# Decay attention in a sixteen-layer hybrid network: the norm and routing steps in other slots

## The chip, the cores and the metric

The program runs on one core of one Trainium2 chip. The metric is the device time of one execution in microseconds (us). Times come as a median over runs, and one execution was recorded by the hardware profiler. The engines are TensorE (PE, with its weight loads listed as PEld), VectorE (DVE), ScalarE (ACT), GpSimd (POOL) and SyncE (SP), which issues most of the transfers. Each engine takes its instructions in program order and waits on semaphores for the others.

## The reference, cut to what matters

The network has sixteen layers. Each one adds `f(layernorm(x))` to `x`, where `x` holds 4096 tokens of 128 channels. The change concerns the decay attention (layer 1, part b) and, inside its loop, the first half of the mixture of experts (MoE) that follows it.

```python
# decay attention: 16 heads of 8 channels, groups of T = 256 tokens
q = (x @ Wq.T + bq).reshape(B, T, H, hd)          # k and v likewise
scores = jnp.einsum('bqhd,bkhd->bhqk', q, k) * scale
decay = jnp.exp(-alpha * jnp.abs(idx[:, None] - idx[None, :]) * DT)
attn = jax.nn.softmax(scores * decay, axis=-1)
out = jnp.einsum('bhqk,bkhd->bqhd', attn, v).reshape(B, T, D)
return out @ Wo.T + bo
...
# the MoE that follows: the best 2 of 8 experts for each token
logits = jnp.einsum('nc,ec->ne', xt, gate_w)
top_vals, top_idx = jax.lax.top_k(logits, TOP_K)
top_w = jax.nn.softmax(top_vals, axis=-1)
```

## The kernel before, in words

`x` lies in SBUF with channels on partitions and is worked on in 8 chunks (`NCH`) of 512 tokens; a chunk holds two groups of 256 tokens. `decay` (L2952) prepares data and a list of steps, and hands them to `small_stage` (L2797), which writes the order of every engine by hand: it counts slots, and what it records in a slot goes into the engines' queues in just that order. Nothing is reordered later.

**One item per slot.** A chunk has 8 items, two groups times four blocks of 128 queries by 128 keys, so item n of chunk c is slot n = 8c to 8c+7. In slot n the loop records, in this order:

1. `score(n)`: four matmuls on PE into four PSUM banks, then `evict` (L2970). For an even slot VectorE multiplies the four banks by the decay table (`pt<-ps,dec`) and the exponential over the whole tile is left for the next slot. For an odd slot ScalarE takes the exponential straight from the four banks (`pt<-ps`). The odd slots take queries and keys that GpSimd has scaled before (`qx`, `kx`).
2. The exponential left from slot n-1 (`pt<-pt`, on ScalarE, so always in an odd slot).
3. The steps that have become due in this slot (`later`, L2816). Where several are due, the leading steps described below come first, then `join`, `turn` and `out`.
4. `weigh_by_head(n-3)`: 32 small matmuls with the values. After each second item the result is copied out as `raw`, by ScalarE or VectorE in turn, always in an even slot. It is transposed and divided (`turn`, `rd` and `o`) one slot later. The two halves are brought together (`join`, `ot`) and, for the second group, multiplied by Wo and added to x by VectorE (`out`, L2905) in slot 8c+13.
5. The steps of chunks to come: `project` (q and k) at 8c-6, `values` at 8c-5, `queries` at 8c-4 and 8c (`qz`), `keys_by_edge` (`kx`) at 8c-3, `queries_by_edge` (`qx`) at 8c-2 and 8c+2, `guard` (two reductions, `peaks`) at 8c+1, and three steps of the norm of x (`norm_x_step`, L1811): a centring matmul with a copy on ScalarE and a square on GpSimd; a mean matmul with a logarithm and an exponential on ScalarE (`nrs`); the scaling on VectorE (`ha<-ha,nrs`). Chunks 0 to 4 were normed by the stage before, so here only chunks 5 to 7 have these three.

PE takes its banks from a ring of six ("s") for everything but the weighing, so that a matmul waits until the bank used six allocations earlier has been read.

**The leading steps.** The stage after the attention is the MoE, so `out(c)` also makes due the eleven steps of `Sending.steps` (L3639) for its chunk, one per slot in the kernel before: three of the norm (centre with copy and square on ScalarE; `nrs` on ScalarE; `ha` on VectorE), `compare` (L3660, a matmul for the logits, then VectorE), `choose` (L3679, thirteen small VectorE instructions), `place` (L3707, small matmuls and five VectorE instructions), `turn` (L3730, four transposes and two copies on ScalarE into `out`), and four `scatter` steps (L3739) of two indirect DMAs each, recorded on GpSimd (L3743). With the last chunk's steps the loop runs on after the last item, up to slot 80. Then `table` is made and the stage of the experts begins; its first `x<-rows` transfer on SP's queue reads what the scatters wrote.

PE's order is therefore fixed in each slot: a matmul that waits for VectorE or ScalarE also holds everything recorded behind it.

Of the kernel before, what the change touches and what calls it, by code (L numbers as in the profile page):

```python
# [21 lines left out]
NCH = NT // CH  # L22
# [1627 lines left out]
class Fast(Net):  # L1650
# [1143 lines left out]
            w["bv"].rearrange("p (h d) -> p h d", h=16)[:, None].broadcast_to([P, 4, 16, 8]), ALU.add,  # L2794
        )

    def small_stage(self, w, units, steps, tiles, evict, finish=None, group=1):  # L2797

# [7 lines left out]
        with ExitStack() as st:  # L2808
            p = self.stage(st, "sm", 1)
# [1 line left out]
            pts, po, ots, os, rests, due = {}, {}, {}, {}, {}, {}  # L2811
            lead = self.lead(p, "s", spread=True)
            first = min(at for at, _ in steps) - 3 * group
            steps = [(first + i * group, lambda c, i=i: self.norm_x_step(p, c, i, "s")) for i in range(3)] + list(steps)

            def later(n, i, f, c):  # L2816


                for _ in range(i):
                    n += 1 if group == 1 or n % group < group - 2 else group - n % group  # L2820
                due.setdefault(n, []).append((order.index(f) if f in order else 0, f, c))
# [13 lines left out]
            def weigh(n, slot):  # L2835
                c, b, it, jt, kind = items[n]
                vz = tiles(c, b, it, jt)[2]
                if n % len(units) == 0:
                    po[0] = self.bank("o")
                pt = pts.pop(n)  # L2840
                first, last = n % len(units) == 0, n % len(units) == len(units) - 1
                for u in range(4):
                    for r in range(4):
                        cc = slice(32 * r, 32 * r + 32)
                        nc.tensor.matmul(
                            po[0][cc, it * P : it * P + P], vz[:, u, cc], pt[:, r, u], start=first and u == 0,
                            stop=last and u == 3, skip_group_check=True,
                        )
                if last:
                    if b == 0:  # L2850
                        ots[c] = p.tile([P, CH], F32, tag="ot", name="ot", bufs=2)
                    finish(c, b, ots[c][:, b * T : b * T + T], po[0])
                    if b == 1:
                        later(slot, 1, out, (slot, c))
# [38 lines left out]
            def join(args):  # L2893
                slot, n = args
                c, b, *_ = items[n]
                if b == 0:
                    ots[c] = p.tile([P, CH], F32, tag="ot", name="ot", bufs=2)
                pt = self.bank("s")
                for it in range(2):
                    self.tr(pt[:, it * P : it * P + P], os.pop((c, b, it)))  # L2900
                self.act(ots[c][:, b * T : b * T + T], pt[:, :T], AF.Copy)
                if b == 1:
                    later(slot, 3, out, (slot, c))

            def out(args):  # L2905
                slot, c = args
                pz = self.bank("s")
                self.mm(pz, w["Wo"], ots.pop(c))
                x = self.x[:, self.chunk(c)]
                if "bo" in w:  # L2910
                    self.stt(x, pz, w["bo"], x, ALU.add, ALU.add)
                else:
                    self.tt(x, x, pz, ALU.add)
                for i, f in enumerate(lead):
                    later(slot, (2 if finish else 4) + i, f, c)

            order = [None, join, turn, out]
            with self.share(s=6, o=2), self.tc.manual_schedule():
                self.logs()
                n = first  # L2920
                while n < len(items) + 3 * group or due:
# [13 lines left out]
                    for at, f in steps:  # L2935
                        c, u = divmod(n - at, many)
# [15 lines left out]
    def decay(self, w):  # L2952


        h0 = self.ha
        nc = self.nc
        with ExitStack() as st:
            p1 = self.stage(st, "d1", 1)
            p2 = self.stage(st, "d2", 2)
            na = p1.tile([P, 1], F32, tag="na", name="na")  # L2960
            self.ts(na, w["alpha"], -1.0, ALU.mult)
            dec = p1.tile([P, P], F32, tag="dec", name="dec")
            self.act(dec, w["lag"][:, :P], AF.Exp, scale=na)
            edge = p1.tile([P, T], F32, tag="edge", name="edge")
            self.act(edge, w["edge"], AF.Exp, scale=na)
            bad = p1.tile([P, 1], F32, tag="bad", name="bad")
            self.ts(bad, w["alpha"], 0.0, ALU.is_lt, 1e30, ALU.mult)
            vzs = self.with_ones(p1, 2)

            def evict(kind, pt, ps):  # L2970
                if kind:
                    for r in range(4):
                        self.act(pt[:, r].rearrange("p h t -> p (h t)"), ps[r], AF.Exp, scale=8.0**-0.5)
                    return
                for r in range(4):
                    self.tt(pt[:, r], ps[r].rearrange("p (h t) -> p h t", h=4), dec[:, None, :].broadcast_to([P, 4, P]), ALU.mult)
                flat = pt.rearrange("p r h t -> p (r h t)")
                return lambda: self.act(flat, flat, AF.Exp, scale=8.0**-0.5)

            qs, ks, kxs, qzs, qxs = {}, {}, {}, {}, {}  # L2980

            def project(c):
                for n, held in (("q", qs), ("k", ks)):
                    pq = self.bank("s")
                    self.mm(pq, w["W" + n], h0[:, self.chunk(c)])
                    held[c] = p2.tile([P, CH], F32, tag=n, name=n)
                    self.act(held[c], pq, AF.Identity, bias=w["b" + n])

            def values(c):
                self.values_by_head(w, vzs[c % 2], self.chunk(c))  # L2990

            def queries(c, b):
                qzs[c, b] = self.masked_copy(p1, qs[c], b)

            def keys_by_edge(c):
                kxs[c] = p2.tile([P, CH], F32, tag="kx", name="kx")
                self.gt(self.bt(kxs[c]), self.bt(ks[c]), self.twice(edge), ALU.mult)

            def queries_by_edge(c, b):
                qxs[c, b] = p1.tile([P, 4, T], F32, tag="qx", name="qx", bufs=3)  # L3000
                self.gt(qxs[c, b], qzs[c, b], edge[:, None, :].broadcast_to([P, 4, T]), ALU.mult)

            def guard(c):
                self.guard(DECAY, c, qs[c], ks[c])
                if c == 0:
                    at = DECAY * 2 * PEAKS
                    self.tt(self.peaks[:, at : at + 1], self.peaks[:, at : at + 1], bad, ALU.add)

            def tiles(c, b, it, jt):
                kk, qq = (ks, qzs) if it == jt else (kxs, qxs)  # L3010
                j = b * T + jt * P
                return kk[c][:, j : j + P], qq[c, b][:, :, it * P : it * P + P], vzs[c % 2][:, 2 * b + jt]

            steps = [
                (1, guard), (-6, project), (-5, values), (-4, lambda c: queries(c, 0)), (-3, keys_by_edge),
                (-2, lambda c: queries_by_edge(c, 0)), (0, lambda c: queries(c, 1)), (2, lambda c: queries_by_edge(c, 1)),
            ]
            units = [(0, 0, 0), (0, 1, 1), (1, 1, 0), (1, 0, 1)]
            self.small_stage(w, units, steps, tiles, evict)

    def guard(self, stage, c, q, k):
        self.peak(stage, 0, c, q)
# [823 lines left out]
```

## Time and profile before

| | |
|---|---|
| median of 3 runs | 4256.13 us (4253.08 to 4257.88) |
| profiled execution | 4251.58 us, of it span 4249.8 us |
| decay attention with its leading steps | about 2200 to 2514 us of the span |
| `peaks<-q` of chunks 2 to 7 (slot 8c+1) starts at | 2265.45, 2299.67, 2337.21, 2374.87, 2412.54, 2446.74 us |
| one `qx` on GpSimd | 2.37 us |
| one `rows<-out,idx` issue on GpSimd | 0.97 to 1.05 us, 1.27 from start to start |

The distance between two `peaks<-q` is the time of one chunk in the steady part of the loop: 34.22 us, 37.54, 37.66, 37.67 and 34.20. The three longer ones hold the norm of chunks 5, 6 and 7. In a timeline each line gives the start, the length, the engine, the line of the kernel and operation, and in brackets the idle time of that engine just before with what ended it; lines of one kind are merged, so the idle time inside a merged line is not shown, and its length shows it instead.

### The profile page before, as it was taken

To read this page: it belongs to the slowest core of one execution; us is meant where nothing else is said; L and a number is where in the kernel's file an instruction comes from. 1 tells how busy PE (TensorE), PEld (TensorE's weight loads), DVE (VectorE), ACT (ScalarE), POOL (GpSimd) and SP (SyncE) were. 2 spreads that over 40 slices of the span, in tenths; PEclk is the share of its full clock that TensorE was granted. 3 is DMA by queue.
4 is the path that set the end of the run, shared out by engine and by line. 5 is a ranking of instruction groups with operands and counts; after the bars stand their busy time and mean duration, and the time that the engine had idled before them with its cause. 6 is when DMAs were issued, how large, how long until landed. Compare 5 with 4: busy or idle time off the path is not lost. (4 is left out here: it accounts for less than half of the span.)

```text
span 4249.8 us, 73853 instructions
## 1 busy us (share of the span) xinstructions
PE 3860.8 (91%) x28998; PEld 2207.7 (52%) x28998; DVE 2557.6 (60%) x4503; ACT 2327.2 (55%) x4741; POOL 1852.0 (44%) x1632
## 2 busy tenths in 40 slices
PE   7999999998899999995989979888999999899878
PEld 3555466464465456553965459643444344455333
DVE  4775577364477477555336643565788687486474
ACT  6665466554766456553447634444555455774432
POOL 4664365232565166316433334454555455311251
PEclk9999999988999999997999979999999999999989
DMA  1800000000000000002930049100000000000000
GB/s 61 343 1 1 11 1 1 20 1 1 20 1 1 1 4 2 1 1 83 330 125 12 17 137 316 61 19 16 1 1 1 3 1 1 16 2 18 6 0 21
DMA packets 78404, 176.43 MB, mean 42 GB/s; under 512 B 12606, under 2 KB 39108, under 8 KB 77920
## 3 DMA queue, kind: packets, MB, share of 16 engines
q1 hardware_dynamic: 65568, 148.40, 10.1%
q0 software_dynamic: 9120, 18.51, 1.2%
q8 instruction: 231, 3.78, 0.4%
q10 hardware_dynamic: 3360, 4.72, 0.3%
q14 instruction: 125, 1.02, 0.1%
HBM read 118.28 MB, written 54.20 MB: 41 GB/s over the span
## 5 line engine op out<-in xcount | busy, mean ns | idle before, releaser
L528 ACT ACTIVATE pt<-ps 128x512 f32<-128x512 f32 x640 | 340.0, 600 | 327.7 <-PE ps L504 326.4
L504 PE MATMUL ps<-hb,w 128*128 128x512 f32 (+1 forms) x960 | 458.7, 611 | 6.9 <-issue 3.3
L504 PE MATMUL ps<-w,hb 128*128 128x512 f32 (+2 forms) x896 | 403.4, 571 | 27.9 <-DVE t L531 20.9
L534 POOL TENSOR_TENSOR t<-t,t 128x512 f32<-128x512 f32 x256 | 319.3, 1268 | 160.8 <-DVE t L531 101.2
L531 DVE TENSOR_TENSOR t<-ps,tab 128x512 f32<-128x512 f32 x512 | 317.5, 681 | 83.8 <-ACT sq L528 80.3
L534 POOL TENSOR_TENSOR t<-t,ss 128x1024 f32<-128x1024 f32 x128 | 243.5, 1903 | 218.9 <-ACT ss L528 217.6
L504 PEld LDWEIGHTS ps<-hb,w 128*128 128x128 f32 (+1 forms) x960 | 178.0, 190 | 263.7 <-issue 224.3
L528 ACT ACTIVATE qkt<-ps 128x512 f32<-128x512 f32 x256 | 140.5, 595 | 309.0 <-PE ps L508 308.4
L531 DVE TENSOR_TENSOR u<-u,ps 128x384 f32<-128x384 f32 (+1 forms) x206 | 121.8, 595 | 287.9 <-PE ps L508 182.9
L531 DVE TENSOR_TENSOR ot<-ps,rd 128x512 f32<-128x512 f32 (+2 forms) x224 | 143.2, 639 | 232.0 <-ACT rd L528 232.0
L534 POOL TENSOR_TENSOR nsq<-ha 128x512 f32<-128x512 f32 x112 | 122.9, 1097 | 320.4 <-ACT ha L528 308.6
L504 PEld LDWEIGHTS ps<-w,hb 128*128 128x128 f32 x896 | 155.5, 192 | 185.4 <-issue 113.6
L534 POOL TENSOR_TENSOR both<-pt 128x1024 f32<-128x1024 f32 x64 | 151.2, 2362 | 200.0 <-DVE pt L531 164.3
L504 PE MATMUL ps<-nsq,ct 128*128 128x512 f32 x368 | 201.0, 629 | 36.0 <-POOL nsq L534 32.1
L504 PE MATMUL ps<-ot,w 128*128 128x512 f32 x448 | 213.6, 611 | 16.8 <-DVE ot L531 9.0
L504 PE MATMUL ps<-xt,w 128*128 128x128 f32 x1704 | 221.0, 280 | 1.5 <-ACT xt L528 1.5
L2199 POOL DMA_INDIRECT back<-y,x x142 | 138.9, 978 | 184.2 <-ACT y L528 90.4
L504 PE MATMUL ps<-u,w 128*128 128x512 f32 (+1 forms) x448 | 215.4, 605 | 3.4 <-POOL u L534 3.4
L528 ACT ACTIVATE u<-ps,w 128x512 f32<-128x512 f32 x160 | 107.8, 685 | 183.8 <-PE ps L504 181.3
L504 PEld LDWEIGHTS ps<-xt,w 128*128 128x128 f32 x1704 | 204.8, 194 | 2.9 <-ACT xt L528 2.9
L528 ACT ACTIVATE nrs<-ps,ct 128x512 f32<-128x512 f32 x208 | 139.8, 683 | 101.8 <-PE ps L504 95.9
L3743 POOL DMA_INDIRECT rows<-out,idx x128 | 125.8, 982 | 155.1 <-ACT out L528 105.7
(362 smaller groups left out, 8937.9 us busy)
## 6 DMA issues: line engine op xcount, KB each, us to landing
w<-in_moe_x SPq DMA_DIRECT2D x142, 533.0 KB
rows<-t SPq DMA_DIRECT2D x64, 520.0 KB
x<-rows SPq DMA_DIRECT2D x142, 65.0 KB
w<-in_local_f SPq DMA_DIRECT2D x8, 659.5 KB
y<-back ACTq DMA_DIRECT2D x16, 256.0 KB
y<-back SPq DMA_DIRECT2D x16, 256.0 KB
w<-in_local_f SPq DMA_DIRECT2D x4, 658.5 KB
back<-y,x POOLq DMA_INDIRECT x142
```

Source lines behind the costliest of these rows:

```text
L504: self.nc.tensor.matmul(out, lhsT, rhs, start=start, stop=stop)
L528: self.nc.scalar.activation(out, in_, func, **kw)
L531: self.nc.vector.tensor_tensor(out, a, b, op)
L534: self.nc.gpsimd.tensor_tensor(out, a, b, op)
L2199: nc.gpsimd.indirect_dma_start(views[i], bass.IndirectOffsetOnAxis(ap=x[:, C : C + 1].bitcast(I32), axis=0), y, None, bounds_check=2 * NT ...
L3743: nc.gpsimd.indirect_dma_start(views[(c * 2 + k) * 4 + t], bass.IndirectOffsetOnAxis(ap=idx[:, k, t : t + 1], axis=0), out[:, k, t], None,)
```

## The change

`small_stage` takes two further arguments. `norm_at` names the slots of the three norm steps (before: three consecutive slots ending with the one before the earliest step, 8c-9, 8c-8, 8c-7; now 8c-10, 8c-8, 8c-7). `lead_at` names the distance of each of the eleven leading steps from the slot in which the chunk's last item is weighed, 8c+10 (before: 4 to 14, one slot after the other). It holds for chunks 0 to 6; the last chunk keeps the old distances. Only `decay` hands them over. In slots: norm of the MoE 8c+14, 16, 17 (before 14, 15, 16), `compare` 19 (17), `choose` 21 (18), `place` 23 (19), `turn` 24 (20), scatters 25 to 28 (21 to 24). No instruction is added or taken away.

```diff
-    def small_stage(self, w, units, steps, tiles, evict, finish=None, group=1):
+    def small_stage(self, w, units, steps, tiles, evict, finish=None, group=1, norm_at=None, lead_at=None):
...
             first = min(at for at, _ in steps) - 3 * group
-            steps = [(first + i * group, lambda c, i=i: self.norm_x_step(p, c, i, "s")) for i in range(3)] + list(steps)
+            norm_at = norm_at or [first + i * group for i in range(3)]
+            first = min(norm_at)
+            steps = [(norm_at[i], lambda c, i=i: self.norm_x_step(p, c, i, "s")) for i in range(3)] + list(steps)
...
                 for i, f in enumerate(lead):
-                    later(slot, (2 if finish else 4) + i, f, c)
+                    later(slot, lead_at[i] if lead_at and c < NCH - 1 else (2 if finish else 4) + i, f, c)
...
-            self.small_stage(w, units, steps, tiles, evict)
+            self.small_stage(
+                w, units, steps, tiles, evict, norm_at=(-10, -8, -7), lead_at=(4, 6, 7, 9, 11, 13, 14, 15, 16, 17, 18),
+            )
```

## The prediction

> **What bounds the kernel now.** The page first, for the engines over the whole span; then busy time by stretches of 34 us, about one chunk; then PE's timeline of the loop, and VectorE's and GpSimd's beside it where PE stands still.
>
> ```profile
> PE 3860.8 (91%) x28998; PEld 2207.7 (52%) x28998; DVE 2557.6 (60%) x4503; ACT 2327.2 (55%) x4741; POOL 1852.0 (44%) x1632
> ...
> 2302.00:2336.00 34.00, 31.08 (x370) 17.36 (x373) 21.23 (x52) 23.86 (x38) 15.31 (x12) 0.95 0.05 17
> ```
>
> PE leads everywhere: 31.08 of 34 us here, VectorE 21.23, ScalarE 23.86. But "busy" includes matmuls held up between their parts, so I price each slot's work from starts in undisturbed slots: score 1.07 us, weighing 1.01, turning `raw` 0.53, join 0.37, Wo 0.96, the two norm matmuls 1.05 and 0.96, logits 0.9, place 0.35, the MoE's turn 0.5, projection 1.92, values 1.07. Eight scores, eight weighings, four turns, two joins and one of each other make 27.3 us per chunk, against 34.2 from `peaks<-q` to `peaks<-q`. Seven us are lost, and they sit in few places. With s for slot modulo 8, this is s = 2 and 3 of chunk 3, PE's timeline:
>
> ```profile
> 2301.72 2.78 PE L504 MATMUL ps<-qx,kx 32*128 32x512 f32 x8
> 2304.89 0.19 PE L504 MATMUL ps<-both,before 128*128 128x32 bf16 x1 [0.40 <-DVE both L538]
> 2304.93 0.32 PE L504 MATMUL ps<-both,ones 128*128 128x24 bf16 x7
> 2306.96 0.91 PE L508 MATMUL ps<-ct,raw 128*128 128x128 f32 x4 [1.71 <-ACT pt L528]
> 2307.80 1.94 PE L2866 MATMUL ps<-pt,vo 128*32 128x128 f32 x32
> 2309.66 1.58 PE L504 MATMUL ps<-w,ha 128*128 128x128 f32 x8
> 2311.17 1.14 PE L504 MATMUL ps<-qz,k 32*128 32x512 f32 x8
> ```
>
> From 2301.72 to 2311.17 are 9.45 us for 4.03 us of work (1.07+0.35+0.53+1.01+1.07). VectorE and GpSimd at that time:
>
> ```profile
> 2296.55 1.92 DVE L531 TENSOR_TENSOR ahead<-lg 128x256 f32<-128x256 f32 x1
> ...
> 2300.85 2.47 DVE L531 TENSOR_TENSOR pt<-ps,dec 128x512 f32<-128x512 f32 x4
> 2303.24 0.41 DVE L3683 TENSOR_REDUCE rank<-ahead 128x32 f32<-128x256 f32 x1
> ...
> 2306.13 0.69 DVE L639 COPY raw<-ps 128x512 f32<-128x512 f32 x1
> ...
> 2295.82 2.37 POOL L534 TENSOR_TENSOR qx<-qz,edge 128x1024 f32<-128x1024 f32 x1 [2.71 <-ACT pt L528]
> ```
>
> `compare` (s=1) makes the even slot's eviction late, so the odd slot's fourth bank comes free late; then `choose` (2303.24 to 2306.13, 2.9 us) stands before the copy of `raw`, and PE waits for that copy. The bracket names ScalarE's `pt`, but the copy ends just before. Afterwards PE is slow for some 4 us (weighing 1.94 for 1.08). The loss is 5.4 us.
>
> Two smaller losses stand where a chunk is normed, three times:
>
> ```profile
> 2329.49 1.12 PE L504 MATMUL ps<-nsq,ct 128*128 128x512 f32 x2 [0.82 <-POOL nsq L534]
> ...
> 2337.43 1.96 PE L504 MATMUL ps<-ha,w 128*128 128x512 f32 x4 [0.98 <-DVE ha L531]
> ```
>
> [...] `ahead` takes 1.92 us under `qx` and 0.42 otherwise, ending 0.28 us after it. [...] about 2.1 us idle, then 4 us slow. [...]
>
> **The change, part by part.** No instruction changes; the order of all engines but SP does.
>
> *Removed (A).* `choose` leaves the even slots, and `compare` leaves s=1, where it met `qx`. Five times 9.38 to 9.45 us for 4.03 are 5 x 5.4 = 27.0. A sixth (2446.88 to 2456.85, 9.97 us, own work 2.96 as it has no values) gives 7.0. Together 34.0.
>
> *Removed (B).* The norm's centring goes two slots ahead of its mean, and `compare` no longer stands before its scaling: 3 x 0.82 and 0.98+1.10+1.11 = 5.6.
>
> *Removed (C).* s=0 is so short (2.45 us) that the next score waits for a bank: 4.39 us for 3.53 at 2293.33, three times, 2.4. In the new order s=0 also has the turn and the mean, 3.9 us. Removed in all: 42.0.
>
> *Added (a): ScalarE in s=0 and 1.* s=0 now holds the MoE's `out` (0.97 from start to start), `nrs` (0.74+0.54), `ot` 0.3, `raw` 0.5, `qz` 0.8. With t0 the start of s=0's score, ScalarE is still at s=7's exponentials until t0+2.15, so `raw` ends at t0+5.25, and turning it, at t0+4.98 on PE, waits 0.47; s=1's evictions start at t0+6.0 and the next score's fourth bank costs 0.2. With the chunk's own `nrs` (1.3 more) the evictions start at about t0+7.3, after which the bank costs 0.9. Two chunks at 0.7 and three at 0.9: 4.1.
>
> *Added (b): `choose` in s=5* stands before `turn`'s and `out`'s VectorE work. It starts after s=4's eviction and `qz`, 4.15 us after s=4's score begins (1.15 until the banks are full, 2.4, 0.6). Its 2.9, then `rd`, `o` (0.5) and the addition to x (0.75) end at 8.3. s=6's score begins at 6.7 (2.45 and 0.7 bank wait for s=4, 3.54 for s=5), so the centring matmul could go at 7.77 and waits some 0.65. Behind it on PE stand the weighing and all of s=7. And `qx` (due in s=6) starts as soon as that `qz` is done, where before it was queued behind scatters: it holds `choose`'s `tensor_tensor`s until 2.37+0.28 us later, 1.5 us on top. In the three chunks with a norm (slots 29, 37, 45) GpSimd's `nsq` is queued ahead of `qx` and waits for s=6, so there is no meeting; slot 61 has no `qx` any more. So 4 x 0.65 and 2 x 2.2 = 7.0. After 2.2 us idle PE may be slow: nothing to 1.4 each (0.9 on the weighing, 0.5 on the values, above); I take 0.7, as the gap is one and not two: 1.4.
>
> *Added (c).* `compare` now meets the last pair (slot 59), which has no projection to cover it; a bank wait of 0.6 stays.
>
> *Added (d): the tail.* After the last item chunk 7's chain sets the end:
>
> ```profile
> 2483.91 0.97 POOL L3743 DMA_INDIRECT rows<-out,idx  x1 [14.29 <-ACT out L528]
> ...
> 2493.29 0.63 ACT L528 ACTIVATE nrs<-nrs 128x512 f32<-128x512 f32 x1
> ...
> 2502.81 0.96 POOL L3743 DMA_INDIRECT rows<-out,idx  x1 [9.03 <-ACT out L528]
> ...
> 2514.30 0.35 SPq L2165 DMA_DIRECT2D x<-rows  x1
> ```
>
> Chunk 6's scatters started at 2483.91 and were over before chunk 7's at 2502.81; the first `x<-rows` waits for the last. Now chunk 6's `turn` is in slot 72, behind chunk 7's `nrs` (over at 2493.9). `compare` in slot 67 also costs some 1.2 us ahead of `rd`. So GpSimd starts at about 2496.1 and has 16 issues at 1.27, to 2516.4, instead of 2512.7: 3.7 us, which nothing covers, because SP's loads for the experts are in line behind that `x<-rows`. `choose` and `place` of chunk 6 fit into the tail's idle VectorE (3.1 us before the addition, 6.8 before `ha`).
>
> The extra first slot (-10) is empty for chunk 0, normed earlier: nothing.
>
> Sum: 42.0 - (4.1+7.0+1.4+0.6+3.7 = 16.8) = 25 us less. Against the profiled execution 4251.6 - 25 = 4226.6; the median of the runs stands 4.5 above it, so 4231.
>
> **Rivals.**
> 1. *The delay moves from s=3 to s=6.* `choose` is held by `qx` in all six chunks and PE goes slow each time: 6 x (2.2+1.4) = 21.6 in place of 8.4, gain 12, 4244. For it: `qx` now follows `qz` at once. Against: `nsq` ahead of it in three chunks.
> 2. *(a) and (b) are hidden by slack I don't see*: only (c), (d) and the 0.65s stay, 42.0-0.6-3.7-2.6 = 35, 4221. For it: ScalarE has 10 us free per chunk.
> 3. *Slower.* If GpSimd comes late to `kx`, `kx` (1.27) and `qx` hold `choose` one after the other: 0.65+1.27+2.37+0.28 = 4.6 us idle before the centring, then twice the slow stretch's 1.4: 7.4 per chunk, 44.4 in all. With (a), (c), (d), 8.4, that is 10.8 more than removed: 4267. It decides from 5.6 us per chunk on (33.6/6). Against: `kx` needs k, done two slots earlier, and the scatters end before.
>
> **How the numbers follow.** The forecast has 0.65 (about 4222 to 4241), rival 2 0.12, rival 1 0.14, rival 3 0.09. A measurement of this kernel can tell about 0.2%, 8.5 us. Rival 1 lies half within that bound: faster 0.65+0.12+0.06 = 0.83, same 0.08, slower 0.09. The range goes down to 4215, past rival 2, as (a) and (b) could vanish whole, and up to 4247, rival 1 with half a us more in each of six chunks; what is left out is rival 3 and the edges. The forecast's own range is 4222 to 4241.
>
> **What would show it.** `peaks<-q` distances of about 31 to 32 us in all steady chunks; at s=3 a score of 1.14 us and no wait for `raw`; on PE a wait for `x` ahead of the centring matmul, longer where `choose` lies under `qx`; the first `x<-rows` 16 scatters after chunk 7's `nrs`. Wrong if s=6 loses over 5 us per chunk, or if ScalarE's `pt` starts more than 3 us after s=1's score.

## The result, and the profile after

| | before | after |
|---|---|---|
| median | 4256.45 us (4 runs, 4253.08 to 4257.88) | 4230.2 us (4 runs, 4228.95 to 4232.05) |
| profiled execution | 4251.58 us | 4230.16 us |
| first score of the attention to the score of slot 63 | 263.4 us | 232.1 us |
| slot 63's score to the first `x<-rows` | 46.9 us | 48.3 us |
| sum of the eight slots s = 3 | 64.0 us | 33.7 us |
| sum of the eight slots s = 6 | 24.0 us | 33.3 us |

The ratio is 0.994, with a 95% interval of 0.9928 to 0.9952: 26 us less. A "slot" is measured from the start of PE's score to the start of the next one. By the trace the stage became 29.9 us shorter, but the profiled executions differ by only 21.4: the after execution reached the first score 8.3 us later, through stages in which nothing had changed. In a second pair of profiles it reached it 1.5 us earlier, so this is scatter between executions. The profiled "before" lay 4.9 us under the median of its runs. The stage is therefore compared from its own first score throughout.

The engines' busy times of the page, and a window of 32 us that is about one chunk (span, then busy us and instruction counts of PE, PEld, DVE, ACT and POOL, then clock, DMA share and GB/s):

```profile
PE 3853.1 (91%) x28998; PEld 2201.8 (52%) x28998; DVE 2557.5 (60%) x4503; ACT 2326.0 (55%) x4741; POOL 1854.5 (44%) x1632
...
2337.00:2369.00 32.00, 31.30 (x384) 16.91 (x383) 25.21 (x61) 25.22 (x40) 15.10 (x12) 1.00 0.06 19
```

Instruction counts and the engines' shares of the span are those of before. The change hardly shows here: over the whole span PE's "busy" falls by 7.7 us, because it was 13.5 us higher ahead of the stage. From the first score to the first `x<-rows` it falls from 263.8 to 244.9 us; matmuls that were stretched by a wait, or ran slowly after one, had counted as busy (of the 4.21 us from 2306.96 to 2311.17 in the profile before, 4.21 are busy, at a mean clock of 0.59). The change shows in the timeline of the slot that had taken 9.45 us, s = 3 of chunk 3, PE:

```profile
2306.10 1.14 PE L504 MATMUL ps<-qx,kx 32*128 32x512 f32 x8
2307.17 1.06 PE L504 MATMUL ps<-w,ha 128*128 128x8 f32 x8
2308.08 0.63 PE L508 MATMUL ps<-ct,raw 128*128 128x128 f32 x4
2308.65 1.08 PE L2868 MATMUL ps<-pt,vo 128*32 128x128 f32 x32
2309.66 1.16 PE L504 MATMUL ps<-w,ha 128*128 128x128 f32 x8
2310.74 1.14 PE L504 MATMUL ps<-qz,k 32*128 32x512 f32 x8
```

No bracket is left: each matmul follows the one before it. The score takes 1.14 us where it took 2.78, there is no wait for `raw`, and the weighing is at 1.08 instead of 1.94. The slot is 4.64 us for 4.64 us of work. All five such slots read 4.65.

What was paid for it stands in s = 6, here chunk 2, PE, then VectorE and GpSimd:

```profile
2286.52 1.14 PE L504 MATMUL ps<-qz,k 32*128 32x512 f32 x8
2289.70 1.13 PE L504 MATMUL ps<-x,ct 128*128 128x512 f32 x2 [2.03 <-DVE x L543]
2290.75 1.08 PE L2868 MATMUL ps<-pt,vo 128*32 128x128 f32 x32
...
2284.97 1.70 DVE L531 TENSOR_TENSOR rank<-rank,won 128x32 f32<-128x32 f32 x1
...
2288.90 0.74 DVE L543 SCALAR_TENSOR_TENSOR x<-ps,w,x 128x512 f32<-128x512 f32 x1
...
2284.25 2.37 POOL L534 TENSOR_TENSOR qx<-qz,edge 128x1024 f32<-128x1024 f32 x1 [6.84 <-DVE qz L538]
```

`rank<-rank,won` is 128 x 32 elements and takes 0.19 us elsewhere. Here it takes 1.70: it started while `qx` ran and ended just after it (2286.67 against 2286.62). Everything behind it is 1.5 us late, so x too, and PE waits for x. Slot 54 is as long (5.24 us, as here); in the three chunks with a norm it is about 0.5 us, and in slot 62 next to nothing.

### The profile page after: what moved, and what is told of

It is laid out like the page before. It is cut to its first block, busy times and chain, and to the rows that moved or that the text cites. A ratio compares the mean times of both kernels' runs of the same rounds, so it can differ in the third digit from the quotient of the medians.

```text
span 4228.4 us, 73859 instructions
## 1 busy us (share of the span) xinstructions
PE 3853.1 (91%) x28998; PEld 2201.8 (52%) x28998; DVE 2557.5 (60%) x4503; ACT 2326.0 (55%) x4741; POOL 1854.5 (44%) x1632
## 5 line engine op out<-in xcount | busy, mean ns | idle before, releaser
L504 PE MATMUL ps<-nsq,ct 128*128 128x512 f32 x368 | 203.1, 635 | 31.7 <-POOL nsq L534 27.3
L504 PE MATMUL ps<-ha,w 128*128 128x512 f32 x320 | 178.5, 680 | 11.7 <-ACT f L528 10.2
```

The costliest lines, as they stand in the source:

```text
L504: self.nc.tensor.matmul(out, lhsT, rhs, start=start, stop=stop)
```

## The experiments

The first four ran on a chip on which the kernel before took 4280.8 us (median of 37 runs); for the others it took 4253.4 and 4254.7. All edits are against the kernel after; "before again" is the kernel before with four more lines that do nothing. `lead_at` holds the distances from slot 8c+10, so its fifth entry, 11, is the choice in slot 8c+21 (s = 5). "Loop" is first score to slot 63's score, "end" is from there to the first `x<-rows`.

| kernel | loop, us | end, us | median, us | ratio to before (95%) |
|---|---|---|---|---|
| norm half alone | 272.5 | 45.0 | 4275.54 | 0.9989 (0.9981 to 0.9998) |
| routing half alone | 262.3 | 55.7 | 4275.34 | 0.999 (0.9981 to 0.9999) |
| choice in s4 | 246.8 | 54.7 | 4260.84 | 0.9953 (0.9939 to 0.9967) |
| choice in s6 | 270.0 | 58.5 | 4288.73 | 1.0021 (1.0013 to 1.0028) |
| before again | 264.3 | 44.1 | 4253.91 | 1.0 (0.9992 to 1.0009) |
| after again | 231.7 | 48.3 | 4223.84 | 0.9933 (0.9916 to 0.995) |
| choice in s7, placing in s1, turn in s2, tail | 239.7 | 45.5 | 4231.14 | 0.9948 (0.9931 to 0.9965) |
| chunk 6 on old distances ("tail") | 231.8 | 45.3 | 4220.59 | 0.9924 (0.9906 to 0.9943) |
| norm half alone, again | 262.9 | 47.6 | 4255.94 | 1.0002 (0.9995 to 1.0008) |
| routing half alone, again | 237.1 | 48.7 | 4230.96 | 0.9945 (0.9927 to 0.9963) |
| tail, turn in s2 | 231.1 | 44.3 | 4221.11 | 0.9924 (0.9908 to 0.9941) |
| tail, choice in s4 | 228.7 | 47.9 | 4221.11 | 0.992 (0.9903 to 0.9937) |

### The halves on the first chip

```diff
 norm half alone
-                w, units, steps, tiles, evict, norm_at=(-10, -8, -7), lead_at=(4, 6, 7, 9, 11, 13, 14, 15, 16, 17, 18),
+                w, units, steps, tiles, evict, norm_at=(-10, -8, -7),
 routing half alone
+                w, units, steps, tiles, evict, lead_at=(4, 6, 7, 9, 11, 13, 14, 15, 16, 17, 18),
```

> Only the chunk's own norm steps stand in the new slots (8c-10, 8c-8, 8c-7); the eleven leading steps stay one per slot as before. Theory (the gain comes from VectorE's choose and compare leaving the places ahead of work that PE waits for): only the three waits of 0.82 us for nsq go, 2 to 4 us less than before, and the slots 8c+3 stay at about 9.4 us. Rival (the norm steps carry the gain): 10 us or more less than before.

> Only the leading steps stand in the new slots; the chunk's own norm stays at 8c-9, 8c-8, 8c-7. Theory: almost all of the gain, but qx is now queued on GpSimd ahead of nsq in the three chunks with a norm, so that it holds choose there too: slots 30, 38 and 46 (the own norm's centring is not in them any more) show a wait for x of about 2 us in place of 0.5, 4.5 us more than the whole change, some 22 us less than before. Rival (nsq's place in GpSimd's queue has nothing to do with it; the hold is something else): those slots wait 0.5 us as in the whole change, and the time is that of the whole change within 2 us.

The norm's half gained 5 us, with an interval from 1 to 8. The routing's half gained 5 us as well, far too little. Its trace has idle time of PE that the profiles of before and after do not have. PE in the end part of the routing half, while GpSimd issues its scatters:

```profile
2490.59 2.80 PE L2868 MATMUL ps<-pt,vo 128*32 128x128 f32 x49
2494.36 0.44 PE L2868 MATMUL ps<-pt,vo 128*32 128x128 f32 x5 [0.97 <-issue]
2495.79 0.43 PE L2868 MATMUL ps<-pt,vo 128*32 128x128 f32 x4 [1.00 <-issue]
2497.21 1.10 PE L2868 MATMUL ps<-pt,vo 128*32 128x128 f32 x4 [0.99 <-issue]
```

"issue" is idle time in which PE waited for nothing that the profile shows. A run of 64 like matmuls, 3.45 us without a break in the kernel after, is cut up here. Over the stage such gaps sum to 13.7 us in the routing half, 2.6 in the norm half, 11.9 with the choice in s4 and 15.5 with it in s6. The gain of a half could not be read from this chip, and the kernel before had no profile from it.

### The place of the choice

```diff
-                w, units, steps, tiles, evict, norm_at=(-10, -8, -7), lead_at=(4, 6, 7, 9, 11, 13, 14, 15, 16, 17, 18),
 in s4
+                w, units, steps, tiles, evict, norm_at=(-10, -8, -7), lead_at=(4, 6, 7, 9, 10, 13, 14, 15, 16, 17, 18),
 in s6
+                w, units, steps, tiles, evict, norm_at=(-10, -8, -7), lead_at=(4, 6, 7, 9, 12, 13, 14, 15, 16, 17, 18),
```

> The whole change, with choose one slot earlier, in an even slot (8c+20), where VectorE takes it after the eviction and ahead of qz instead of behind qz. Theory: qx cannot start before qz, so choose is not held; slots 22 and 54 take about 3.7 us in place of 5.25, everything else stays: 3 us less than the whole change, and no stall at slot 21, because raw of that slot is copied by ScalarE. Rival (VectorE's steps must stay out of even slots): the stall of some 3 to 5 us per chunk is back, 15 to 30 us more than the whole change.

> The whole change, with choose one slot later, in the even slot 8c+22, where VectorE's own copy of raw stands behind it. Theory: the copy comes 2.9 us late, PE waits some 2.7 us for it in each of six slots 8c+23, perhaps with up to 1.4 us of slow PE after it, while the waits for x in slots 8c+22 (6 us in all) go: 10 to 19 us more than the whole change. Rival (even slots are alike): the same as with choose in 8c+20. Rival (VectorE's sum per chunk decides, not its place): within 2 us of the whole change.

Both expectations were set against the whole change, which was not run on this chip; s6 came out 28 us above s4. One slot later, in s6, brings the stall back: slots 31, 39 and 47 take 8.8 us for the 2.87 of the kernel after, slots 23 and 55 5.7 and 6.1, and the kernel is slower than before. PE in slot 23, then PE and VectorE around slot 31:

```profile
2302.47 0.18 PE L504 MATMUL ps<-both,before 128*128 128x32 bf16 x1 [0.93 <-DVE both L538]
2304.55 0.63 PE L508 MATMUL ps<-ct,raw 128*128 128x128 f32 x4 [1.73 <-DVE at L531]
...
2339.14 0.32 PE L504 MATMUL ps<-both,ones 128*128 128x24 bf16 x7
2343.91 1.08 PE L508 MATMUL ps<-ct,raw 128*128 128x128 f32 x4 [4.46 <-DVE at L531]
2344.93 1.94 PE L2868 MATMUL ps<-pt,vo 128*32 128x128 f32 x32
...
2340.11 2.15 DVE L531 TENSOR_TENSOR lg<-lg,sel 128x32 f32<-128x32 f32 x1
...
2343.08 0.68 DVE L639 COPY raw<-ps 128x512 f32<-128x512 f32 x1
```

In slot 23 nothing holds the choice, and PE loses 2.8 us, about what the choice takes. In slot 31 the choice, lengthened by `nsq` and then by `qx` (2.15 us for 0.19), stands ahead of `raw`'s copy, and PE starts to turn `raw` 0.15 us after that copy ends at 2343.76. The bracket names `at`, the instruction that VectorE did next. This is the stall of the kernel before, in another slot. The choice in s4, though it is an even slot, has no such stall: slots 20 and 21 keep 2.45 and 4.16 us. So it is not the parity that matters but what stands behind the choice: in s4 nothing that PE is soon waiting for.

### Before and after once more, and two further orders

```diff
 choice in s7, placing in s1, turn in s2, tail
-                w, units, steps, tiles, evict, norm_at=(-10, -8, -7), lead_at=(4, 6, 7, 9, 11, 13, 14, 15, 16, 17, 18),
+                w, units, steps, tiles, evict, norm_at=(-10, -8, -7), lead_at=(4, 6, 7, 9, 13, 15, 16, 17, 18, 19, 20),
 this kernel and "tail" (chunk 6 on the old distances)
-                    later(slot, lead_at[i] if lead_at and c < NCH - 1 else (2 if finish else 4) + i, f, c)
+                    later(slot, lead_at[i] if lead_at and c < NCH - 2 else (2 if finish else 4) + i, f, c)
```

> The kernel before with four comment lines in it, so that its lines have the numbers of the kernel after; nothing of its work differs. It is run for what the two experiments with one half of the change need, a profile of the unchanged kernel from the chip that is being used. Theory (the lengths of slots follow from the order of the steps alone): ratio 1.00; the stretch from the first score to that of slot 63 is 263 us, with slot 3 of every chunk at 9.4 us after the first chunk. Rival (a delay that belongs to the chip lengthens the slots around the scatters of any order): the stretch is 270 us or more, and the surplus stands in slots 0 to 3 of a chunk, where ScalarE is idle for about 2 us between two of its copies with no engine named that it waits for.

> The kernel after, unchanged, once more. Theory (order alone): ratio 0.994, the stretch from the first score to slot 63's is 232 us, slots 3 of the chunks at 4.65 us. Rival (a delay of the chip): 238 to 245 us, the surplus in slots 0 to 3 of a chunk and between slot 63 and the first load of the tail, without the 9.4-us slots coming back.

> The kernel after with the choice of the best two moved from slot s5 to s7, the placing of the tokens from s7 to s1 of the next chunk, and the turn and the four steps of scatters two slots on; chunk 6 keeps the old distances as chunk 7 does. Theory (of the time that the kernel after still loses, 6.1 us is VectorE held by the edge's product of qx in s6, where the weighing's evictions stand behind the choice; about 6 us is ScalarE short of time in s0 and s1): x is evicted before the choice starts, so s6 of slots 22, 30, 38, 46 and 54 loses its 0.6 to 2.1 us, a gain of about 5.5 us; the turn leaves s0, a gain of 2 us or so; chunk 6's scatters come earlier, 1 us. Together 8 us less than the kernel after, a ratio of 0.992 against before. Rival (the hold only moves: in s7 ct and qz stand behind the choice, and the copy of raw behind ct): slots 23, 31, ... grow by what slots 22, 30, ... lose, and the time is that of the kernel after, 0.994, or more.

> The kernel after, but chunk 6 keeps the old distances of its steps, as chunk 7 does. Theory (the end of the stage is set by the row of scatters of the last two chunks on GpSimd): from slot 63's score to the first load of rows is 46.9 us as in the kernel before, 1.4 us less than in the kernel after; but with the choice of chunk 6 in s0 and the scatters in s3 of the last chunk, slots 56 to 59 change too: slot 59 may come back to 9 us or so, since in that chunk the scatters stand ahead of nothing else of ScalarE's that was moved. In that case the time is 3 to 5 us above that of the kernel after, ratio 0.995. Rival (chunk 6's steps are away from the choice of any later chunk, so slot 59 stays under 5 us): the time is 1 to 2 us below that of the kernel after, 0.9935.

On this chip PE has no "issue" gap at all in the stage, and nearly every slot repeats that of the first profiles within 0.1 us (slot 2 varies by 0.4). Here order alone explains the slots of both kernels; the long ones of the first chip go with that chip.

The choice in s7 lost its wait in s6 as expected (27.2 us for 33.3 over the eight slots) and gave more back elsewhere: s0 +2.0, s1 +1.7, s2 +3.7, s3 +7.0. PE, VectorE and GpSimd in chunk 3:

```profile
2325.73 0.41 PE L508 MATMUL ps<-ct,o 128*128 128x128 f32 x2 [1.41 <-DVE o L531]
...
2321.21 2.29 DVE L531 TENSOR_TENSOR rank<-rank,ct 128x32 f32<-128x32 f32 x1
...
2331.52 2.35 DVE L531 TENSOR_TENSOR ha<-ha,nrs 128x512 f32<-128x512 f32 x1
...
2321.09 2.36 POOL L534 TENSOR_TENSOR qx<-qz,edge 128x1024 f32<-128x1024 f32 x1
2330.52 2.80 POOL L534 TENSOR_TENSOR qx<-qz,edge 128x1024 f32<-128x1024 f32 x1 [7.08 <-DVE idx L3731]
```

The choice met the `qx` of s6, so `o` was late and PE waited 1.41 us. In s1 a second `qx`, no longer kept back by scatters, held the scaling of the norm (2.35 us for 0.68). About half of the 7.0 us in s3 is slot 59 alone (7.2 us for 3.56): there `qx` holds `place`, now in s1 (one instruction at 1.93 us for 0.23), so that the next eviction is late and the score waits for its banks. The kernel is 7 us slower than the kernel after, where 8 us faster were expected. The rival was right: the hold moves with the work.

The tail kernel leaves the slots alone (slot 59 3.56 us, no 9-us slot) and is 3.0 us shorter at the end: the rival was right about the slots, and both had the end at 1 to 2 us only.

### The halves again, and two small repairs

```diff
 tail, turn in s2
-                w, units, steps, tiles, evict, norm_at=(-10, -8, -7), lead_at=(4, 6, 7, 9, 11, 13, 14, 15, 16, 17, 18),
+                w, units, steps, tiles, evict, norm_at=(-10, -8, -7), lead_at=(4, 6, 7, 9, 11, 13, 16, 17, 18, 19, 20),
 tail, choice in s4
+                w, units, steps, tiles, evict, norm_at=(-10, -8, -7), lead_at=(4, 6, 7, 9, 10, 13, 14, 15, 16, 17, 18),
```

The two repairs have the tail's line as well.

> The norm's half alone, as in the first experiment, for its slots on a chip whose PE shows no idle time without a releaser. Theory: the waits of 0.82 us ahead of the first `ps<-nsq,ct` and of 0.98 to 1.11 us ahead of `ps<-ha,w` go, in three chunks, 5.6 us; the stalls of 5.4 us in the slots s3 stay; the stretch from the first score to slot 63's is 258 us, ratio 0.9987. Rival (centring two slots earlier displaces something in s6): slots 30, 38 and 46 grow by as much, and the ratio is 1.000.

> The routing's half alone, as in the second experiment. Theory (the small gain of the second experiment, 5 us, is due to that chip, where PE stood idle for 13.7 us of the stage without a releaser): those gaps are absent, the stalls in s3 are gone, and what is given back is the choice under qx in s6 of the chunks with a norm (slots 30, 38, 46 at 5.2 to 6.5 us for 3.14, 7 us together) and the norm's two waits, which stay; the stretch from the first score to slot 63's is 242 to 246 us, ratio 0.9955. Rival (the two halves need each other: without the norm's move the routing's gives back nearly all): 255 us or more, ratio 0.998 or above.

> The kernel after with the turn two slots later, in s2 instead of s0, the scatters two slots later with it, and chunk 6 on the old distances. Theory (ScalarE is short of time in s0 and s1, because `out` and the two `nrs` stand there behind one another, and s2 has room): slots s0 of the later chunks go from 5.25 to 4.3 us, five chunks, 4 to 5 us less than the run with the tail alone, ratio 0.991. Rival (the 0.97 us of `out` only move with it, into s2 and s3, where in the run with the choice in s7 slots s2 and s3 were 0.7 and 0.8 us longer): the same time as the run with the tail alone, 0.9925, or up to 4 us more.

> The choice in slot s4 and chunk 6 on the old distances, together, and nothing else against the kernel after. Theory (what is left of the hold by qx lies in the two chunks without a norm, and the tail's 3 us are the scatters of chunk 6 in front of chunk 7's): slots 22 and 54 go from 5.24 to 3.73 us, the tail from 48.3 to 45.3 us; 6 us less than the kernel after, ratio 0.992 or less, and none of the long slots s1 and s3 that the choice in s4 showed on the first chip (25, 33, 41, 49 and 57 at 4.3 to 5.6 us), as these are gaps without a releaser. Rival (those long slots come from the choice in s4 itself): they are back, and the ratio is 0.995 or more.

In the loop the norm's half alone gains 1.3 us (264.3 to 262.9), where 6 were expected; the routing's alone gains 27.2, more than was expected; both gain 32.6. In each figure 0.4 us is slot 2, which varies by as much between executions. The routing's move carries the change, and the norm's is worth little without it. PE and VectorE of the norm half alone, in slot 42:

```profile
2376.82 1.96 PE L504 MATMUL ps<-ha,w 128*128 128x512 f32 x4 [0.99 <-DVE ha L531]
...
2372.78 2.48 DVE L531 TENSOR_TENSOR ahead<-ahead,ct 128x256 f32<-128x256 f32 x1
...
2375.99 0.68 DVE L531 TENSOR_TENSOR ha<-ha,nrs 128x512 f32<-128x512 f32 x1
```

The wait for `ha` stays, because `compare` (`ahead`, held by `qx`) is still ahead of the scaling. Of the 2.7 us that the half saves in s0 it loses 2.0 again in s3 and s4, where PE is slow for longer after the old stall: in slots 43 and 44 the turning of `raw` takes 1.09 us, the values 2.08 and the score 1.38, against 0.63, 1.88 and 1.14 in the kernel before.

PE of the routing half alone, in slots 30 and 46:

```profile
2316.64 1.12 PE L504 MATMUL ps<-x,ct 128*128 128x512 f32 x2 [2.03 <-DVE x L543]
2317.69 1.08 PE L2868 MATMUL ps<-pt,vo 128*32 128x128 f32 x32
...
2383.01 1.78 PE L504 MATMUL ps<-x,ct 128*128 128x512 f32 x2 [2.02 <-DVE x L543]
2384.72 1.94 PE L2868 MATMUL ps<-pt,vo 128*32 128x128 f32 x32
```

The norm's own waits (0.82 us for `nsq`, about 1 for `ha`), which the expectation had kept, are gone here too. What the norm's move adds is the order on GpSimd: without it no `nsq` stands ahead of `qx`, so the choice meets it in the chunks with a norm as well: 2.03 us where the kernel after waits 0.52. Slots 30 to 32 and 38 to 40 take 14.2 us instead of 12.9, and 46 to 48 take 15.8, as PE also turns slow there (the weighing 1.94 us for 1.08). Together these are the 5.4 us by which the two halves with each other beat the routing's alone.

With the turn in s2, slots 32, 40 and 48 fell from 5.25 to 4.45 us as the theory said, and 34, 42 and 50 rose from 5.07 to 5.66; slot 54 waited 2.74 us for x instead of 2.03. Net 0.7 us in the loop: the rival's case.

The choice in s4, on a chip without gaps, shows none of the long slots of the first chip. VectorE and PE in chunk 2:

```profile
2280.47 0.19 DVE L531 TENSOR_TENSOR rank<-rank,won 128x32 f32<-128x32 f32 x1
...
2282.40 0.61 DVE L538 TENSOR_SCALAR qz<-q,ct 128x256 f32<-128x256 f32 x2
...
2284.22 1.13 PE L504 MATMUL ps<-x,ct 128*128 128x512 f32 x2 [0.53 <-DVE x L543]
```

`qz`, which lets `qx` start, now comes after the choice, so `qx` cannot hold it: 0.19 us, and the wait for x is 0.53. The loop is 3.0 us shorter than with the choice in s5. This kernel, the tail and the tail with the turn in s2 are some 3 us under the kernel after in their medians, with intervals that overlap; 6 us were expected of this one, but its end is 47.9 us, not 45.3. What the traces show for certain is this 3.0 us in the loop. The three repairs together were not tried.

## Why the prediction was right, step by step

Predicted were 4231 us for the median, 25 us less; measured 4230.2 and 26 less. In the loop the steps said 42.0 - (4.1 + 8.4 + 0.6) = 28.9 us, and the two pairs of traces show 31.3 and 32.6; in the end part 3.7 us more, and they show 1.4 and 4.2. So by the traces the stage lost 29.9 and 28.4 us, not 25, and when both kernels were timed again the medians lay 29.6 us apart. The mechanism was right, and the range was; that the first medians agree to 1 us is in part luck. Neither sign of being wrong showed: s=6 loses at most 2.1 us in a chunk, and ScalarE's `pt` starts 2.2 us after s=1's score.

- **A, the stalls in s3 and slot 59 (34.0):** right, cause and size. All are gone (from `peaks<-q` to `peaks<-q` it is now 30.55, 32.38, 31.92, 31.90 and 30.69 us, where about 31 to 32 were said), and the experiment with the choice in s6 made them again, with the choice ahead of `raw`'s copy. What `compare` ahead of the even slot's eviction added to them (the score of 2.78 us for 1.14) was not tried by itself.
- **B, the norm's waits (5.6):** they are gone but for 0.17 us three times. The prediction gives the first wait (0.82) to the norm's centring and the second (3.2 us in all) to `compare`. Both are gone with the routing's half alone, so the norm's move was not needed for either; the norm half alone, expected at 258 us, kept the second.
- **C (2.4):** the bank wait of 4.39 us slots in s1 is gone. (Three times 4.39 less 3.53 is 2.6.)
- **(a), ScalarE in s0 and s1 (4.1):** seen, about 5.7 us: 1.08 in each of the chunks 4 to 6, 0.95 in chunks 3 and 7, and 0.6 in chunk 2, which the prediction did not count. PE's score of slot 34, ScalarE before it, and VectorE:

```profile
2333.24 2.21 PE L504 MATMUL ps<-qz,k 32*128 32x512 f32 x8
...
2328.40 0.69 ACT L528 ACTIVATE nrs<-ps,ct 128x512 f32<-128x512 f32 x1
...
2331.40 0.63 ACT L528 ACTIVATE nrs<-nrs 128x512 f32<-128x512 f32 x1
2331.94 0.89 ACT L528 ACTIVATE qz<-q,ct 128x256 f32<-128x256 f32 x2
2332.74 2.04 ACT L528 ACTIVATE pt<-ps 128x512 f32<-128x512 f32 x4
...
2324.67 1.97 DVE L3731 CAST idx<-to 128x8 int32<-128x8 f32 x1
```

The two `nrs` and `qz` hold up the evictions of s1 (`pt<-ps`), so the next score waits for its banks. VectorE adds something not foreseen ahead of s0: `idx<-to`, a cast of 128 x 8 elements, takes 1.97 us under `qx` for 0.17 in chunk 2 and ends just after it (2326.64 against 2326.61), and `o` is late by the 0.17 us of B.
- **(c), `compare` in slot 59 (0.6):** it did not occur. Slot 59 is 3.56 us without a wait, and the score after it takes its usual time.
- **(b), the wait for x in s6 (8.4):** mechanism right, size 6.1 (the slots less their own work: 2.11, 2.12, three times 0.60, 0.08). `qx` holds the choice in the two chunks without a norm and not in the three with one, as the sum had it, and the routing half alone shows why. Two terms were too high: slot 62 has no wait to speak of (0.08 for 0.65), and PE did not turn slow (0 for 1.4). In slots 22 and 54 the end of a clock step split the wait (1.46 and 0.58 us, 0.87 and 1.17), and the granted clock stayed at 1.00; see the next point.
- **The slow PE:** taking half was a guess between the ends. The routing half shows both ends: after the wait of 2.02 us in slot 46 the centring took 1.78 us and the weighing 1.94, after the wait of 2.03 us in slot 30 they took 1.12 and 1.08. The granted clock in the profiles of before and after shows a difference between such waits: it changes only at the ends of steps of 3.41 us. Before, in slot 27, 2.10 us of idle lay in one step (2303.76 to 2307.17), and in the next the granted clock was 0.50 and the weighing took 1.94 us. After, the wait of 2.03 us in slot 22 was split at 2289.12 into 1.46 and 0.58 us, the clock stayed at 1.00 and the weighing took 1.08. That it is the share of a wait in one step that decides is an estimate from these.
- **(d), the end (3.7):** mechanism right. Chunk 7's `nrs` on ScalarE, then GpSimd, after:

```profile
2469.61 0.63 ACT L528 ACTIVATE nrs<-nrs 128x512 f32<-128x512 f32 x1
...
2471.00 0.97 POOL L3747 DMA_INDIRECT rows<-out,idx  x1 [10.84 <-ACT out L528]
...
2481.20 0.97 POOL L3747 DMA_INDIRECT rows<-out,idx  x1 [0.30 <-issue]
...
2490.12 0.97 POOL L3747 DMA_INDIRECT rows<-out,idx  x1 [0.30 <-issue]
```

Sixteen issues stand in one row; chunk 7's eight, from 2481.20 on, wait only for chunk 6's. They begin 26.6 us after slot 63's score, in both executions, where the prediction has 28.7. But the size of the loss depends on the kernel before: with its order PE falls slow in the end part in one execution (the mean's matmul in 2.07 us) and not in another (1.13), and its end is 46.9, 44.1 or, with the same order in the norm half, 47.6 us. The tail kernel has the same spread (44.3 to 47.9 over three kernels), so it repairs between 0.4 and 4.0 us.

Rival 1 (held in six chunks, slow each time) fails on the three chunks with a norm; rival 2 (nothing of (a) and (b) on the path) fails on the 2.03-us brackets and the 5.25-us slots; of rival 3, `kx` held not the choice but `compare`, in four chunks (one instruction at 1.72 us for 0.19 in slot 27, one at about 1.65 for 0.42 in slots 35, 43 and 51), and PE waited for none of these: the slots are the ones of 4.65 us.

Taken with measured sizes the loop's sum is 42.0 - 6.1 - 5.7 - 0.5 = 29.7 us, 1.6 and 2.9 less than the traces show. By estimate some 1.5 us of it can be placed: the scores in s5 wait less than before (33.2 us for the eight slots before, 32.5 after), C is 0.2 larger, and the stalls in s3 some 0.6, as the `place` matmuls, priced at 0.35 us, take 0.21 where nothing holds them. The rest is open. (The prices of the own work add up to 27.2 us per chunk, not 27.3; nothing rests on it.)

## What to carry to other kernels

Where the order of engines is written by hand, price a step by what stands behind it on its engine and by the engine that can hold it, not by its own time: with the choice in s6, its 2.9 us ahead of `raw`'s copy cost 2.8 us where nothing held it and 5.9 where `nsq` and `qx` did; with the choice in s4 PE waited about 0.5 us, for x. Put a step that another engine's work can hold ahead of the instruction that releases that work, as the choice ahead of `qz` (there its `rank<-rank,won` took 0.19 us, behind `qz` 1.70). Two edits can be worth more together than apart, here 32.6 us against 1.3 and 27.2, so run the pair before dropping the one that looks idle alone.

## What the runs showed of the hardware

- On one chip of those used PE stood idle for 2.6 to 15.5 us per stage with no releaser, mostly near rows of indirect DMAs on GpSimd, and in three of the four kernels ScalarE for 1.9 to 4.7 us at a time (its releaser is given as "remote"); in the other profiles PE has no such gap in this stage. The kernel before was 24 to 27 us slower on it. DMA transfers of the kind `instruction` took no longer on it (a median of 0.95 us in the routing half, 1.03 in the same kernel on another chip), and only two of the 35 gaps hold the end of one. The cause is open.
- How long GpSimd held an instruction of VectorE did not go by the size of what was held: 128 x 32 elements took 1.70 us for 0.19, 128 x 8 elements 1.97 for 0.17. They ended 0.05 and 0.03 us after the `qx` beside them.
- The granted clock of PE changed only at the ends of steps of 3.41 us in the profiles of before and after. From 2190 us to the end of the stage these two have ten steps at full clock with 1.97 us or more of idle PE, and each was followed by one at half clock. With 1.46 us of idle the clock stayed at full once; after 0.75, 1.41 and 1.67 us it fell. Matmuls stretched by a wait count as busy here, so the true idle time of such a step is not known.
